# Attention and experts in one kernel: products as two column halves, experts' work in even shares, and the last batch's turns on TensorE

## The chip, the cores and the metric

The kernel runs on one core of one Trainium2 chip. The metric is the device time of the whole kernel in microseconds, as the median of several runs. All data are 32-bit floats.

The core has engines that run side by side and wait for each other by semaphores: TensorE (PE, with its weight loads PEld), VectorE (DVE), ScalarE (ACT), GpSimd (POOL) and SyncE (SP), which here only issues transfers. A "record" is one instruction in the profile; a 32-bit matmul leaves two records, each with a weight load of its own.

## The reference

The input x is 8 batches of 512 tokens with 256 channels. It is normalised over the channels. Two things are computed from the normalised tokens and added to x.

```python
xn = _layernorm(x, axis=-1)
x = x + attention(xn, qkv_w, out_w, bias_p, bias_a, rope_freqs) + experts(xn, Wg, w1, w2)

# attention: 16 heads of 64
qkv = (x @ qkv_w.T).reshape(Bb, Ss, 3, H, D)
q = _rope(q, c, s); k = _rope(k, c, s)
scores = einsum('bhqd,bhkd->bhqk', q, k) * SCALE
kb = -p * log1p(a * dist)                    # bias by distance, one p and a per head
attn = softmax(scores + kb[None], axis=-1)
out = einsum('bhqk,bhkd->bhqd', attn, v)  ->  out @ out_w.T

# experts: 16, each takes at most 256 tokens; a token goes to its best one
gate = softmax(xr @ Wg); idx = argmax(gate); loc = place of the token in its expert's queue
h = relu(einsum('ecm,emf->ecf', dispatched, w1))     # 256 -> 1024
expert_out = einsum('ecf,efm->ecm', h, w2)           # 1024 -> 256
combined = expert_out[idx, min(loc, C - 1)] * (gates_s * (loc < C))[:, None]
```

## The kernel before

**Steps and duos.** The 16 heads form 4 groups of 4, and a *step* s is one group on one batch: 32 steps, group by group over the 8 batches. A step has two *pairs* of heads. For each pair there are four blocks of 128 queries (`qc`); a pair with one block is a *unit*, and two units are a *duo* (`d`). So a step has four duos (`dd` 0 to 3), and the main loop runs over 128 duos. The order on every engine is the order in which the program issues instructions; no scheduler changes it.

**What one duo issues**, in this order:

- `project_qk` (matmuls L574) makes q or k of one pair for the next step: 128x128 weights, 512 columns of data. DVE shuffles the result (L578), ACT copies it (L583), and POOL rotates it by three operations (L587 to L589).
- `score` (L624) for the units of the next duo. Each head has its own 64 rows of the array. DVE adds the bias and reduces (L635), ACT takes the exponential and sums it (L639).
- `attend` (L716) in every second duo (`dd` 1 and 3), for a pair whose exponentials were turned some four duos before. Each head has 64 columns of the array. `attended` (L726) multiplies by the inverse sums on DVE.
- `project_out` (L755) for step s-2 in `dd` 0, twice; `project_v` (L601) in `dd` 0 and 1. The output is gathered in a tile y that is loaded from and stored to memory once in a step (`load_y`, `store_y`).
- `turn` (L648): DVE transposes blocks of 32x32 in the tile z of exponentials. When a pair is complete, `move` (L661) issues 16 transfers on SP's queue that put the blocks in their places (`pt<-z`), and three more (`rd`, `rb`) that spread the inverse sums.
- From duo 44 or so on, pieces of the experts' work (`expert_work`). An expert has 8 pieces of about the same size: four of `expert_hidden` (L519) and four of `expert_out` (L534). `expert_in` transposes an expert's tokens by TensorE (L504). How many pieces a duo takes is written out by hand:

```python
            for _ in range((1, 1, 4, 2 + s % 2)[dd]):
```

Weights of the experts are loaded by SP too; calls that issue them wait in a list `later`, which the next duo empties after `attend`.

**PSUM.** The pool `ps_mm` has two buffers for all products, `ps_sc` four for scores, `ps_av` and `ps_po` one each.

**The end.** From duo `late` (108) on, experts' results are gathered on POOL (L769), weighted on ACT (`weigh`, L781) and added on POOL (`combine`, L785). The last step's second pair is not moved by transfers: `turn_last` scales z by the inverse sums on DVE (L684), TensorE transposes it in blocks of 128x128 (L690), and ACT copies the result (L691). The first pair of the last step goes the ordinary way, through `turn`, `move` and `attend`, and is attended only when the loop is over. Then come `attend_last` (L705), the last `project_out`, and two stores (L983).

Of the kernel before, what the change touches and what calls it, by code (L numbers as in the profile page):

```python
# [37 lines left out]
def attention_and_experts(  # L38
# [138 lines left out]
    def rotation(stage):  # L177

        c1, c2 = 6.28125, 0.00193500518798828125
        c3 = 2.0 * math.pi - c1 - c2  # L180
        magic, edge = 12582912.0, 3.1415925
        n, r, away = two[0][:, 1, :], two[1][:, 0, :], two[1][:, 1, :]
        if stage == 0:
            nc.vector.tensor_scalar(n, ang, 0.5 / math.pi, magic, ALU.mult, ALU.add)
            nc.vector.tensor_scalar(n, n, magic, None, ALU.subtract)
            nc.vector.scalar_tensor_tensor(r, n, -c1, ang, ALU.mult, ALU.add)
        if stage == 1:
            nc.vector.scalar_tensor_tensor(r, n, -c2, r, ALU.mult, ALU.add)
            nc.vector.scalar_tensor_tensor(r, n, -c3, r, ALU.mult, ALU.add)
            nc.vector.tensor_scalar(r, r, edge, -edge, ALU.min, ALU.max)  # L190
            nc.scalar.activation(sin_t, r, AF.Sin, scale=sgn)

            nc.scalar.activation(away, r, AF.Abs)
            nc.scalar.activation(cos_t, away, AF.Sin, bias=quarter, scale=-1.0)


    mv = const.tile([P, NT, 2], F32, name="mv")
# [313 lines left out]
    def expert_hidden(e, f2):  # L511
        if f2 == 0:
            held["hT", e] = ffn["a"].tile([P, F // P, CAP], F32, tag="hT", name=f"hT_{e}")
        hT, xdT = held["hT", e], held["xdT", e]
        ph = ps_mm.tile([P, 2, CAP], F32, tag="mm", name=f"ph_{e}_{f2}")
        for i in range(2):
            fc = 2 * f2 + i
            for mc in range(2):
                nc.tensor.matmul(  # L519
                    ph[:, i, :],  # L520
                    held["w1", e, fc // 4][:, mc, (fc % 4) * P : (fc % 4 + 1) * P],
                    xdT[:, mc, :],
                    start=(mc == 0), stop=(mc == 1),
                )
        nc.scalar.activation(hT[:, 2 * f2 : 2 * f2 + 2, :], ph, AF.Relu)  # L525

    def expert_out(e, quarter):
        c, half = divmod(quarter, 2)
        hT = held["hT", e]
        if quarter == 0:  # L530
            held["po", e] = ps_po.tile([P, 2, DM], F32, tag="po", name=f"po_{e}")
        po = held["po", e]
        for fc in range(half * 4, half * 4 + 4):
            nc.tensor.matmul(  # L534
                po[:, c, :], hT[:, fc, c * P : (c + 1) * P], held["w2", e, fc // 4][:, fc % 4, :],
                start=(fc == 0), stop=(fc == F // P - 1),
            )
        if quarter == 3:
            ot = ffn["a"].tile([P, 2, DM], F32, tag="eo", name=f"eot_{e}")
            nc.scalar.copy(ot, po)  # L540
            later.append(
                lambda: nc.sync.dma_start(
                    eo[e * CAP : (e + 1) * CAP, :].rearrange("(c p) m -> p c m", p=P), ot
                )
            )

    def expert_work():
        for e in range(E):
            for f2 in range(4):
# [5 lines left out]
                yield  # L555
            for quarter in range(4):
                expert_out(e, quarter)
                if quarter == 2 and e + 1 < E:
                    expert_in(e + 1)
                if quarter == 3 and e + 1 < E:  # L560
                    later.append(lambda e=e: load_w2(e + 1))
                yield


    qk: dict = {}
    vals: dict = {}

    def project_qk(s, pair, part, turn_too=True):
# [2 lines left out]
        ps = ps_mm.tile([P, S], F32, tag="mm", name=f"qk_{s}_{pair}_{part}")  # L571
        c0 = part * GC + pair * P
        for mc in range(2):
            nc.tensor.matmul(  # L574
                ps, wq[:, mc, c0 : c0 + P], xnTs[s][:, mc, :], start=(mc == 0), stop=(mc == 1),
            )
        sh = rope.tile([P, S], F32, tag="sh", name=f"sh_{s}_{pair}_{part}", bufs=3)
# [13 lines left out]
    def project_v(s, i2):  # L591
# [6 lines left out]
        for i in range(2):  # L598
            c0 = (2 * i2 + i) * P
            for mc in range(2):  # L600
                nc.tensor.matmul(  # L601
                    ps[:, i, :], xnTs[s][:, mc, c0 : c0 + P], wq[:, mc, 2 * GC :],
                    start=(mc == 0), stop=(mc == 1),
                )
# [9 lines left out]
    def score(s, pair, qc):  # L614
# [1 line left out]
        g = s // B  # L616
        q, k = qk[s, pair, 0], qk[s, pair, 1]
        if qc == 0:
            zts[s, pair] = zpool.tile([P, TB, TB, 2, TB, 32], F32, tag="z", name=f"z_{s}_{pair}")
            sums[s, pair] = small.tile([P, 2, TB], F32, tag="sums", name=f"sums_{s}_{pair}")  # L620
        sc = [ps_sc.tile([P, S], F32, tag="sc", name=f"sc_{s}_{pair}_{qc}_{j}") for j in range(2)]
        for j in range(2):
# [6 lines left out]
            )  # L629
        st = small.tile([P, 2], F32, tag="st", name=f"st_{s}_{pair}_{qc}")  # L630
        for j in range(2):
            z = zts[s, pair][:, :, :, j, qc, :]
            bias = kb[g * HG + 2 * pair + j][:, :, TB - 1 - qc : 2 * TB - 1 - qc, :]

            nc.vector.tensor_tensor_reduce(  # L635
# [37 lines left out]
        pts[s, pair] = pt  # L673
        norms[s, pair] = rb

    def turn_last(s, pair, qc):

        if qc == 0:
            pts[s, pair] = zpool.tile([P, 2, TB, S], F32, tag="z", name=f"pt_{s}_{pair}")
        rs = small.tile([P, 2], F32, tag="rs", name=f"rs_{s}_{pair}_{qc}")  # L680
        nc.vector.reciprocal(rs, sums[s, pair][:, :, qc])
        for j in range(2):
            zn = rope.tile([P, S], F32, tag="sh", name=f"zn_{s}_{pair}_{qc}_{j}", bufs=3)
            nc.vector.tensor_scalar(  # L684
                zn.rearrange("p (c g k) -> p g c k", g=TB, k=32),
                zts[s, pair][:, :, :, j, qc, :], rs[:, j : j + 1], None, ALU.mult,
            )
            ps = ps_mm.tile([P, TB, P], F32, tag="mm", name=f"zt_{s}_{pair}_{qc}_{j}")
            for kc in range(TB):
                nc.tensor.transpose(ps[:, kc, :], zn[:, kc * P : (kc + 1) * P], ident)  # L690
            nc.scalar.copy(pts[s, pair][:, j, :, qc * P : (qc + 1) * P], ps)  # L691

    oTs: dict = {}
    avs: dict = {}

    def attend_last(s, pair, i2):

        if i2 == 0:
            avs[s, pair] = ps_av.tile([P, S], F32, tag="av", name=f"av_{s}_{pair}")
            oTs[pair] = qkpool.tile([P, S], F32, tag=f"o{pair}", name=f"o_{s}_{pair}", bufs=1)  # L700
        av, c = avs[s, pair], slice(i2 * 2 * P, (i2 + 1) * 2 * P)
        for kc in range(TB):
            for j in range(2):
                c0 = pair * P + j * D
                nc.tensor.matmul(  # L705
                    av[j * D : (j + 1) * D, c], vals[s][:, kc, c0 : c0 + D],
                    pts[s, pair][:, j, kc, c], start=(kc == 0), stop=(kc == TB - 1),
                )
        nc.vector.tensor_copy(oTs[pair][:, c], av[:, c])

    def attend(s, pair):
        avs[s, pair] = av = ps_av.tile([P, S], F32, tag="av", name=f"av_{s}_{pair}")
# [33 lines left out]
            out[b].rearrange("(n p) d -> p n d", p=P) if last else yd[b], ys.pop(s)  # L746
        )

    def project_out(s, i2):
        _, wot = weights[s // B]  # L750
        ps = ps_mm.tile([P, 2, DM], F32, tag="mm", name=f"po_{s}_{i2}")
        for i in range(2):
            c0 = (2 * i2 + i) * P
            for pair in range(2):
                nc.tensor.matmul(  # L755
                    ps[:, i, :], oTs[pair][:, c0 : c0 + P], wot[:, pair, :],
                    start=(pair == 0), stop=(pair == 1),
                )
        y = ys[s][:, 2 * i2 : 2 * i2 + 2, :]
# [40 lines left out]
        )  # L800


    steps = NG * B
    units = [(s, pair, qc) for s in range(steps) for pair in range(2) for qc in range(TB)]
    duos = len(units) // 2
    late = duos - 5 * TB
# [43 lines left out]
    turned_at = {3: 2, 6: 3, 8: 4, 10: 5, 12: 6, 14: 7}  # L850
    routing = route()
    working = begin = None
    for d in range(duos):
        s, dd = divmod(d, TB)
        g, b = divmod(s, B)
        pair, half = divmod(dd, 2)
        final = (s, pair) == units[-1][:2]
        if s + 1 < steps:
            project_qk(s + 1, *divmod(dd, 2))
        if d in turned_at:  # L860
            transpose_normed(turned_at[d])
        if d + 1 < duos:
            score(*units[2 * d + 2])
            score(*units[2 * d + 3])
        was = divmod((d - 5) // 2, 2) if half and d >= 5 else None
        if was:
            attend(*was)
# [13 lines left out]

        if dd == 0 and s > 1:
            project_out(s - 2, 0)
        if d == duos - 1:
            attended(*was)
            project_out(s - 1, 0)
            project_out(s - 1, 1)
            store_y(s - 1, True)
        (turn_last if final else turn)(*units[2 * d])
        if was and d < duos - 1:  # L890
            attended(*was)
        if d == 1:
            turn_logits(0)
# [3 lines left out]
            turn_logits(turned_at[d - 1])  # L897
        if dd in (0, 1):
            project_v(s, dd)
        (turn_last if final else turn)(*units[2 * d + 1])  # L900
        if dd == 1 and 4 <= s + 2 < steps:
            load_normed(s + 2)
        if half and not final:
            move(s, pair)
        if dd == 0 and s > 1:
            project_out(s - 2, 1)
# [26 lines left out]
            expert_in(0)  # L933
            working = expert_work()
        elif working:
            for _ in range((1, 1, 4, 2 + s % 2)[dd]):
                if working and next(working, True):
                    working = None

        assert working is None or d < late  # L940

        if d >= late and s < steps - 1:
            if dd < 2:
                gather(b - 1, dd)
            if dd == 2:
# [28 lines left out]
                bias_tables(g + 1, 0, 1)  # L974
        if b == 0 and g > 0 and dd == 0:
            bias_tables(g, 1, 1)
    attend(s, 0)
    attended(s, 0)
    for i2 in range(2):
        attend_last(s, 1, i2)  # L980
    for i2 in range(2):
        project_out(s, i2)
        nc.sync.dma_start(  # L983
            out[B - 1, i2 * 2 * P : (i2 + 1) * 2 * P].rearrange("(n p) d -> p n d", p=P),
            ys[s][:, 2 * i2 : 2 * i2 + 2, :],
# [50 lines left out]
```

## Time and profile before

| | |
|---|---|
| median of 3 runs | 1260.9 us (1260.34 to 1262.82) |
| the profiled execution | 1259.97 us |
| its span, first to last instruction | 1258.3 us |
| PE busy | 1214.7 us, 97% of the span |
| DVE busy | 892.5 us, 71% |
| ACT, POOL busy | 611.8 us, 618.1 us |
| mean granted TensorE clock | 0.990 |
| PE idle from 1150 to 1200 us | 4.3 of 50 us |
| transfers | 264.15 MB, mean 210 GB/s |

The busy time of PE counts its matmul records, which overlap each other; the gap between the starts of two groups tells more than their length. A row of the chain gives the start in us, the length in us, and the engine with the line and the number of instructions. In a row of the timeline the bracket gives the time for which the engine stood idle before it, and what released it. SPq is the time that SP needs to issue transfers.

The main groups of matmuls, with their shape (rows x columns of the array, then rows x columns of data):

| line | what | shape | records | busy us |
|---|---|---|---|---|
| L624 | scores | 64*128, 64x512 | 1024 | 254.7 |
| L574 | q and k | 128*128, 128x512 | 512 | 246.4 |
| L716 | attention times v | 128*64, 128x512 | 1008 | 232.1 |
| L755 | output product | 128*128, 128x256 | 512 | 124.4 |
| L601 | v | 128*128, 128x256 | 512 | 124.1 |
| L534 | experts, second product | 128*128, 128x256 | 512 | 120.3 |
| L519 | experts, first product | 128*128, 128x256 | 512 | 118.7 |

### The profile page before, as it was taken

The numbers are of one execution on the slowest core, as the hardware profiler recorded it, in microseconds if no ns is written. First come the engines' busy times: TensorE is split into PE (matmuls) and PEld (weight loads), VectorE is DVE, ScalarE is ACT, GpSimd is POOL, SyncE is SP. The second block draws the span as 40 slices with busy tenths as digits, with TensorE's granted clock in tenths as the row PEclk, the third lists the DMA queues.
The fourth block names the chain that finished last, engine by engine and source line by source line (L and its number), as shares of the span: only waits on it lengthen the run. The fifth ranks groups of instructions, "written<-read, shape, count | busy, mean of one in ns | idle before, by whom it ended". The sixth has DMA issues, their size and how long they took to land.

```text
span 1258.3 us, 17383 instructions
## 1 busy us (share of the span) xinstructions
PE 1214.7 (97%) x5070; PEld 669.1 (53%) x5070; DVE 892.5 (71%) x2265; ACT 611.8 (49%) x1425; POOL 618.1 (49%) x614
## 2 busy tenths in 40 slices
PE   8799999999999999999999999999999999998977
PEld 5344444444465656656565665655656554444444
DVE  7988899999966656555656566655665668888762
ACT  6565655566443444335543344443446435555550
POOL 5766754555543444334443344433434335687850
PEclk9899999999999999999999999999999999999988
DMA  4489998888888997778786787877778768889995
GB/s 135 146 219 262 253 252 203 207 218 208 212 240 210 239 265 193 198 198 212 199 232 166 237 202 211 227 196 205 195 196 215 191 166 203 220 229 218 246 232 139
DMA packets 152414, 264.15 MB, mean 210 GB/s; under 512 B 32176, under 2 KB 96448, under 8 KB 152320
## 3 DMA queue, kind: packets, MB, share of 16 engines
q1 hardware_dynamic: 144848, 240.98, 72.5%
q0 software_dynamic: 6368, 20.99, 5.8%
q10 hardware_dynamic: 1104, 1.07, 0.2%
q8 instruction: 41, 0.67, 0.2%
q14 instruction: 53, 0.43, 0.1%
HBM read 99.39 MB, written 31.44 MB: 104 GB/s over the span
## 4 chain that ended last, share of the span: by engine, by line
PE 76%; DVE 8%; DMA 7%; SPq 4%; POOL 2%; ACT 2%; issue 1%; ACTq 0%; DVEq 0%; POOLq 0%
PE sc L624 15%; PE qk L574 14%; PE av L716 14%; PE ph L519 9%; PE po L534 9%; PE v L601 7%; PE po L755 7%; SPq L661 3%; DVE z L635 3%; DMA pt<-z 2%; DVE z L648 2%; DMA rd<-turned 1%; DMA xnT<-xnd 1%; DMA xnd<-xnT 1%; DMA out<-early 1%
## 5 line engine op out<-in xcount | busy, mean ns | idle before, releaser
L587 POOL TENSOR_TENSOR t<-t,cos_t 128x512 f32<-128x512 f32 (+1 forms) x126 | 161.3, 1280 | 537.9 <-ACT t L583 537.4
L639 ACT ACTIVATE z<-z,st 128x512 f32<-128x512 f32 x512 | 363.4, 712 | 35.2 <-DVE st L635 26.0
L635 DVE CUSTOM_DVE_ANT_1 z<-sc,kb 128x512 f32<-128x512 f32 x512 | 322.5, 686 | 29.2 <-PE sc L624 23.8
L648 DVE STREAM_TRANSPOSE z<-z 128x512 f32<-128x512 f32 x504 | 319.9, 682 | 0.0
L624 PE MATMUL sc<-t,t 64*128 64x512 f32 x1024 | 254.7, 616 | 0.7 <-DVE t L589 0.7
L574 PE MATMUL qk<-xnT,wq 128*128 128x512 f32 x512 | 246.4, 604 | 6.5 <-ACT early L781 1.9
L716 PE MATMUL av<-pt,v 128*64 128x512 f32 x1008 | 232.1, 602 | 3.7 <-DMA rb<-rd 1.8
L583 ACT COPY t<-qk 128x512 f32<-128x512 f32 x125 | 73.2, 585 | 330.6 <-DVE sh L578 324.3
L624 PEld LDWEIGHTS sc<-t,t 64*128 64x128 f32 x1024 | 88.3, 186 | 154.1 <-issue 124.3
L578 DVE LOAD_MASK_SELECT sh<-qk x128 | 1.8, 14 | 231.6 <-PE qk L574 224.7
L589 POOL TENSOR_TENSOR t<-t,sh 128x512 f32<-128x512 f32 (+1 forms) x126 | 160.6, 1275 | 9.9
L588 POOL TENSOR_TENSOR sh<-sh,sin_t 128x512 f32<-128x512 f32 (+1 forms) x126 | 161.2, 1279 | 0.0
L716 PEld LDWEIGHTS av<-pt,v 128*64 128x64 f32 x1008 | 67.8, 137 | 159.6 <-issue 131.3
L574 PEld LDWEIGHTS qk<-xnT,wq 128*128 128x128 f32 x512 | 93.8, 191 | 95.2 <-issue 67.5
L755 PE MATMUL po<-wo,o 128*128 128x256 f32 x512 | 124.4, 386 | 0.4 <-ACT t L583 0.2
L601 PE MATMUL v<-wq,xnT 128*128 128x256 f32 x512 | 124.1, 385 | 0.0
L534 PE MATMUL po<-w,hT 128*128 128x256 f32 x512 | 120.3, 383 | 1.0 <-ACT hT L525 1.0
L519 PE MATMUL ph<-xdT,w 128*128 128x256 f32 x512 | 118.7, 382 | 1.4 <-ACT eot L540 1.4
L755 PEld LDWEIGHTS po<-wo,o 128*128 128x128 f32 x512 | 94.4, 190 | 36.9 <-issue 12.6
L601 PEld LDWEIGHTS v<-wq,xnT 128*128 128x128 f32 x512 | 94.7, 190 | 35.8 <-DVE z L648 13.8
L519 PEld LDWEIGHTS ph<-xdT,w 128*128 128x128 f32 x512 | 95.7, 190 | 26.5 <-ACT z L639 4.9
L534 PEld LDWEIGHTS po<-w,hT 128*128 128x128 f32 x512 | 95.2, 190 | 25.3 <-issue 8.7
(147 smaller groups left out, 831.9 us busy)
## 6 DMA issues: line engine op xcount, KB each, us to landing
pt<-z SPq DMA_DIRECT2D x1008, 128.0 KB
w<-in_w SPq DMA_DIRECT2D x64, 512.0 KB
rb<-rd SPq DMA_DIRECT2D x126, 128.0 KB
xnT<-xnd SPq DMA_DIRECT2D x28, 512.0 KB
yd<-y SPq DMA_DIRECT2D x26, 512.0 KB
y<-yd SPq DMA_DIRECT2D x24, 512.0 KB
xrd<-xn POOLq DMA_DIRECT2D x8, 512.0 KB
xnd<-xnT POOLq DMA_DIRECT2D x8, 512.0 KB
```

The source lines that it names most:

```text
L519: nc.tensor.matmul(ph[:, i, :], held["w1", e, fc // 4][:, mc, (fc % 4) * P : (fc % 4 + 1) * P], xdT[:, mc, :], start=(mc == 0), stop=(mc = ...
L534: nc.tensor.matmul(po[:, c, :], hT[:, fc, c * P : (c + 1) * P], held["w2", e, fc // 4][:, fc % 4, :], start=(fc == 0), stop=(fc == F // P ...
L574: nc.tensor.matmul(ps, wq[:, mc, c0 : c0 + P], xnTs[s][:, mc, :], start=(mc == 0), stop=(mc == 1),)
L587: eng.tensor_tensor(t[:, c], ps[:, c], cos_t[:, c], ALU.mult)
L588: eng.tensor_tensor(sh[:, c], sh[:, c], sin_t[:, c], ALU.mult)
L601: nc.tensor.matmul(ps[:, i, :], xnTs[s][:, mc, c0 : c0 + P], wq[:, mc, 2 * GC :], start=(mc == 0), stop=(mc == 1),)
L624: nc.tensor.matmul(sc[j].rearrange("p (g c k) -> p g c k", g=TB, k=32), q[r, qc * P : (qc + 1) * P], k[r, :].rearrange("p (c g k) -> p g c ...
L635: nc.vector.tensor_tensor_reduce(z, sc[j].rearrange("p (g c k) -> p g c k", g=TB, k=32), bias, -0.125, 3.0e38, ALU.add, ALU.min, st[:, j : ...
L639: nc.scalar.activation(z, z, AF.Exp, bias=st[:, j : j + 1], scale=-1.0, accum_out=sums[s, pair][:, j, qc : qc + 1],)
L648: nc.vector.transpose(z, z)
L716: nc.tensor.matmul(av[j * D : (j + 1) * D, :].rearrange("p (a q) -> p a q", q=P), vals[s][:, kc, c0 : c0 + D], pts[s, pair][:, :, kc, j, : ...
L755: nc.tensor.matmul(ps[:, i, :], oTs[pair][:, c0 : c0 + P], wot[:, pair, :], start=(pair == 0), stop=(pair == 1),)
```

## The change

It has three parts.

1. A new function `product` stands in for the single matmul in `project_qk`, `project_v`, `project_out`, `expert_hidden` and `expert_out`. It issues two matmuls, one for each half of 64 columns of the weights, on the same data; the halves fill the two halves of the output's partitions. The transposes keep all 128 columns.
2. The pieces of the experts' work are spread by a running count, so that the last one falls in the last duo before `late`. `expert_in` of the next expert is called from the list `coming`, behind the scores of the duo that follows its piece `quarter` 0; before, it was called at `quarter` 2, among the pieces.
3. The loop ends four duos earlier, and the last step is written out behind it. Both pairs of it are now transposed by TensorE straight from the exponentials (`turn_last`), half of the copies back by ACT and half by DVE, in place. The inverse sums are not multiplied in before: `sums_last` widens them on DVE, `spread_last` turns them by TensorE into the layout of the output, and `attend_last` multiplies by them at the end. So that the keys may keep their order, a copy of the last step's input is reordered by ACT (`reordered`), and v is made from that copy.

```diff
+    def product(o, w, v, start, stop):
+
+        for c in range(2):
+            half = slice(c * D, (c + 1) * D)
+            nc.tensor.matmul(o[half], w[:, half], v, start=start, stop=stop)
...
             for mc in range(2):
-                nc.tensor.matmul(
+                product(
                     ph[:, i, :],
...
             for quarter in range(4):
                 expert_out(e, quarter)
-                if quarter == 2 and e + 1 < E:
-                    expert_in(e + 1)
+                if quarter == 0 and e + 1 < E:
+                    coming.append(e + 1)
...
-    def turn_last(s, pair, qc):
-
-        if qc == 0:
-            pts[s, pair] = zpool.tile([P, 2, TB, S], F32, tag="z", name=f"pt_{s}_{pair}")
-        rs = small.tile([P, 2], F32, tag="rs", name=f"rs_{s}_{pair}_{qc}")
-        nc.vector.reciprocal(rs, sums[s, pair][:, :, qc])
+    def turn_last(s, pair, qc, spare=(ps_po, "po")):
+
+
         for j in range(2):
-            zn = rope.tile([P, S], F32, tag="sh", name=f"zn_{s}_{pair}_{qc}_{j}", bufs=3)
-            nc.vector.tensor_scalar(
-                zn.rearrange("p (c g k) -> p g c k", g=TB, k=32),
-                zts[s, pair][:, :, :, j, qc, :], rs[:, j : j + 1], None, ALU.mult,
-            )
-            ps = ps_mm.tile([P, TB, P], F32, tag="mm", name=f"zt_{s}_{pair}_{qc}_{j}")
-            for kc in range(TB):
-                nc.tensor.transpose(ps[:, kc, :], zn[:, kc * P : (kc + 1) * P], ident)
-            nc.scalar.copy(pts[s, pair][:, j, :, qc * P : (qc + 1) * P], ps)
+            z = zts[s, pair][:, j, qc].rearrange("p g c k -> p g (c k)")
+            pool, tag = spare if j else (ps_mm, "mm")
+            ps = pool.tile([P, TB, P], F32, tag=tag, name=f"zt_{s}_{pair}_{qc}_{j}")
+            for g in range(TB):
+                nc.tensor.transpose(ps[:, g], z[:, g], ident)
+            (nc.vector.tensor_copy if j else nc.scalar.copy)(z, ps)
+
+    def sums_last(s, pair):
+
+        inv = inverse[pair]
+        nc.vector.reciprocal(inv[:, : 2 * TB], sums[s, pair].rearrange("p j c -> p (j c)"))
+        norms[s, pair] = rope.tile([P, 2, TB, D], F32, tag="sh", name=f"wide_{pair}", bufs=3)
+        nc.vector.tensor_copy(
+            norms[s, pair].rearrange("p j c d -> p (j c) d"),
+            inv[:, : 2 * TB].unsqueeze(2).to_broadcast([P, 2 * TB, D]),
+        )
+
+    def spread_last(s, pair):
+
+        wide = norms[s, pair]
+        ps = ps_po.tile([P, S], F32, tag="po", name=f"spread_{pair}")
+        for qc in range(TB):
+            for j in range(2):
+                nc.tensor.matmul(
+                    ps[j * D : (j + 1) * D, qc * P : (qc + 1) * P], wide[:, j, qc, :], ident,
+                    start=True, stop=True,
+                )
+        norms[s, pair] = rope.tile([P, S], F32, tag="rb", name=f"rb_{s}_{pair}")
+        nc.scalar.copy(norms[s, pair], ps)
...
-    for d in range(duos):
+    for d in range(duos - TB):
...
+        if s == steps - 2 and dd == 2:
...
+            reordered = xpool.tile([P, 2, S], F32, tag="xnT", name="reordered")
...
+        while coming:
+            expert_in(coming.pop())
...
-            for _ in range((1, 1, 4, 2 + s % 2)[dd]):
+            share = (1, 1, 4, 2)
+            due = 8 * E * sum(share[k % TB] for k in range(begin + 1, d + 1)) / sum(
+                share[k % TB] for k in range(begin + 1, late))
+            for _ in range(min(4, math.ceil(due - 1e-6) - pieces)):
+                pieces += 1
                 if working and next(working, True):
                     working = None
...
+    s, rest = steps - 1, units[-2 * TB :]
+    xnTs[s] = reordered
+    score(*rest[2])
+    score(*rest[3])
...
+    for unit in rest[:2]:
+        turn_last(*unit)
+    weigh(B - 2)
+    gather(B - 1, 1)
+
+    score(*rest[4])
+    score(*rest[5])
+    attend(s - 1, 0)
+    load_y(s)
+    attended(s - 1, 0)
+    for unit in rest[2:4]:
+        turn_last(*unit)
+    sums_last(s, 0)
...
+    score(*rest[6])
+    score(*rest[7])
+    spread_last(s, 0)
+    attend_last(s, 0, 0, TB)
+    for unit in rest[4:6]:
+        turn_last(*unit)
+    combine(B - 1, ys[s])
+    attend(s - 1, 1)
+    attended(s - 1, 1)
+    turn_last(*rest[6], (ps_sc, "sc"))
+    sums_last(s, 1)
+    turn_last(*rest[7], (ps_sc, "sc"))
+    for i2 in range(2):
+        project_out(s - 1, i2)
+    store_y(s - 1, True)
+    spread_last(s, 1)
+    for i2 in range(2):
+        attend_last(s, 1, i2, 2)
     for i2 in range(2):
-        project_out(s, i2)
+        project_out(s, i2, lasts)
```

## The prediction

> **What bounds the kernel now.** I read the page's engine row and chain first, then stretches of the span, then the chain row by row where it changes, then the end.
>
> ```profile
> PE 1214.7 (97%) x5070; PEld 669.1 (53%) x5070; DVE 892.5 (71%) x2265; ACT 611.8 (49%) x1425; POOL 618.1 (49%) x614
> PE 76%; DVE 8%; DMA 7%; SPq 4%; POOL 2%; ACT 2%; issue 1%; ACTq 0%; DVEq 0%; POOLq 0%
> ```
> TensorE is the bound on average. By stretches (us, then busy time of PE, PEld, DVE, ACT, POOL, then granted clock, DMA share, GB/s):
>
> ```profile
> 200.00:400.00 200.00, 198.42 (x822) 97.48 (x821) 175.76 (x454) 104.35 (x245) 101.12 (x83) 1.00 0.86 218
> 600.00:800.00 200.00, 200.00 (x831) 121.86 (x828) 120.72 (x292) 87.79 (x200) 81.69 (x68) 1.00 0.76 208
> 1150.00:1200.00 50.00, 45.69 (x176) 20.31 (x172) 40.49 (x100) 28.39 (x72) 40.05 (x34) 1.00 0.99 251
> 1225.00:1258.00 33.00, 25.14 (x120) 14.29 (x120) 6.91 (x14) 4.23 (x8) 2.35 (x1) 0.86 0.53 143
> ```
> From 60 to 1119 us PE is never free: only less PE time helps. Near 1150 the DMA share is 0.99 and PE waits for transfers. At the end PE has gaps and a lower clock. Now the chain where PE carries it (start, length, instructions):
>
> ```profile
> 1140.75 1.73 PE v L601 x8
> 1142.47 1.73 PE po L755 x8
> 1144.20 1.72 PE qk L574 x4
> 1145.92 1.92 PE sc L624 x8
> 1147.83 3.58 PE av L716 x16
> 1151.42 1.93 PE v L601 x8
> ```
> The same v group takes 1.73 us behind another full 128x128 group but 1.93 behind av, which uses 64 columns. sc (64 rows) takes 1.92 where its eight records at 0.215 make 1.72; av takes 3.58 where sixteen make 3.44. So each change of the array's shape costs PE 0.20 us, or 0.145 where the weights entered have only 64 columns. Last, PE's timeline at the end:
>
> ```profile
> 1208.16 3.65 PE L716 MATMUL av<-pt,v 128*64 128x512 f32 x16 [0.66 <-issue]
> 1218.10 1.57 PE L690 MATMUL zt<-ident,zn 128*128 128x128 f32 x8 [2.45 <-DVE zn L684]
> 1225.37 1.97 PE L690 MATMUL zt<-ident,zn 128*128 128x128 f32 x8 [5.70 <-ACT pt L691]
> 1227.27 4.37 PE L716 MATMUL av<-pt,v 128*64 128x512 f32 x16
> 1245.64 1.95 PE L705 MATMUL av<-pt,v 128*64 128x256 f32 x16 [0.80 <-DVE o L726]
> ```
> Gaps, and behind them slow groups: the av of 3.65 us takes 4.37 after the 5.70 us gap.
>
> **Part one: products as two halves of 64 columns.** A product of 128 output rows becomes two matmuls on halves of the array's columns. av already has this form: in the starts of its records two stand 7 ns apart and pairs follow every 429 ns, and the full qk records also follow every 429 ns. For 256 columns of data L705 shows 16 records in 1.95 us against 1.93 for eight full v records, both behind other work; pairs follow every 216 ns, full ones every 216. So the work itself costs nothing more, though PE issues 7694 matmul records instead of 5070.
>
> What changes is the number of shape changes. I counted them along PE's instruction order in both kernels. Leaving a 64-column group for a full one: 62 before, 21 after, so 41 x 0.20 = 8.2 us less. Leaving a full group for a 64-column one: 2 before, 32 after, 30 x 0.145 = 4.4 us more; these are the transposes (expert inputs, normed batches, logits), which stay full and used to stand among full products. Score groups followed by 64-column work: 61 before, 104 after, 43 x 0.055 = 2.4 us less; after the logits 8 x 0.055 = 0.4 less. Net 6.6 us less. Expert inputs moved behind sc, out of the experts' work, are in this count at 15 x 0.20 = 3.0 us of loss.
>
> A rule speaks against it. The Trainium skill, "TensorE: Matmul & The Clock Gate", section "What overlaps and what doesn't", says that a weight load runs beside matmuls in flight only if its row group differs. Both halves use all 128 rows, so by the rule their loads would not be hidden. The two 64-column loads of a pair would cost, at the 0.137 us of the av loads' row, up to 0.27 us on each of 2560 pairs: 700 us slower. The starts in L716 and L705, 429 and 216 ns a pair with each pair's loads between, show them hidden. I take the trace. What no row shows is two halves reading the same data at once; its bounds are 0 and the rule's 0.27 us, and I take 0 because av is the same form in all but that.
>
> **Part two: experts' work spread.** The 128 pieces run to the last duo allowed, three duos later than before; PE is full in both stretches, so moving pieces costs nothing. Each step now has the pattern 1, 1, 4, 2, so a new expert always opens a new duo. Before, PE waited twice 0.69 us for an expert's output copy where one expert followed another at once (818 and 862 us): 1.4 us less. Transposes of an expert's input now wait for its gather on POOL, issued two duos earlier; their copy stands on DVE behind four score reductions (4 x 0.61 us), while PE has av or po (1.7 to 3.6 us) and one more PSUM buffer. If that cover fails a step loses under 1 us. SP stores the last expert output just before POOL gathers; POOL then waits a few us with rope work behind it that is needed two duos (14 us) later: 0. The weights of w1 are asked for in duo four and used at the end of the next duo, some 16 us; 1 MB at the 208 GB/s of that stretch is 5 us: 0.
>
> **From 1119 us the gain stops.** There the chain is SP's issues and transfers:
>
> ```profile
> 1176.33 2.94 SPq L661 DMA_DIRECT2D pt<-z  x4
> 1179.93 11.32 SPq L661 DMA_DIRECT2D pt<-z  x12
> 1191.29 1.30 SPq L669 DMA_DIRECT2D rb<-rd  x2
> ```
> Twelve issues took 11.3 us where a free run of them takes 7.50 (the one at 1196.88), and av at 1194.63 waited 1.75 us for rb. The change leaves these queues alone, so PE's 0.5 us a step over 2.5 steps becomes waiting: 1.2 us lost. Up to 1194.63: 6.6 + 1.4 - 1.2 = 6.8 us less.
>
> **Part three: the last batch.** From that av to the end took 63.7 us: 41.8 us of PE work at full pace, 12.1 of gaps, 4.5 from the last matmul to the end (DVE 0.69, transfer 3.8), and the rest, 5.3, is the lower clock. The change removes the last batch's first pair's 16 pt, 1 rd and 2 rb issues on SP (1225.3 to 1237.7), 8 DVE transposes of 0.68 and 8 scalings of 0.48. It adds 32 transposes of 0.109 us (from the xdp group, 0.437 for four), 32 records that spread the sums (1.7 us), two ACT copies that reorder the last input (0.6 each, beside 44% of ACT's time), and 8 copies on DVE of about 0.69 (the row of xdT). PE's work becomes 47.1 us.
>
> Waits on that path: the last pt of the batch before (SP issues it to 1222.96, its buffer was free at 1224.7) is wanted by my sum at about 1225.7 on the same scale, just in time. Single-buffered turns wait for a DVE copy three times at about 0.4: 1.2 us. Other hand-overs, 0.9. The y of the last batch, asked for 12 us earlier on SP, lands and is added with about 6 us to spare. The slow groups stood behind gaps of 2.45 and 5.70 us; none as long is left in my sum, so I expect the full clock, and the 5.3 us go with the 12.1 of gaps. 47.1 + 2.1 + 4.5 = 53.7 against 63.7: 10.0 us less.
>
> **Sum.** 6.8 + 10.0 = 16.8 us from the profiled execution's 1259.97 us (span 1258.3 and 1.7 around it): 1243.2. The profiled run lies 0.9 under the median of 1260.9 and inside the runs' range, so I say 1243.5.
>
> **Rivals.**
> A: transfers hold the end (0.2). If the last pt arrives when it did before, whatever PE saved, av of the batch before waits 6 to 7 us in the new end. For: DMA share 0.99 and the tight meeting above. Against: the queue's backlog begins only near 1119, so it should shift with PE. About 1249.
> B: halves are not free (0.06). If each pair costs over 6.6 ns more than one full product, 2560 pairs eat the whole 16.8 us. At 20 ns, 51 us: 1294. For: same-data reads and 50% more records are shown nowhere. Against: L716 and L705 agree with full products to 1 ns.
> C: the even pattern frees more (0.12): fewer waits on transfers near 1130 to 1195, where PE stood idle 6.2 us, because fewer steps run there without experts. About 1237.
> D: the switch saving isn't real, or new expert waits of 0.5 us in each of 15 steps eat it (0.1): the end alone, about 1250.
>
> **Numbers.** The main case has 0.52, range 1239 to 1248. With A whole and the larger part of C and D the range is 1236 to 1252; outside lie B, the far ends of C and D, and a twelfth or so of the main case. Within 0.2% is what this measurement can't tell from no change, 2.5 us: only a small part of B and D reaches it. Faster 0.92, same 0.02, slower 0.06.
>
> **What would show it.** Right: v behind av 1.73 us; sc still 1.92; po behind sc about 1.87; a steady step without experts 28.9 us instead of 29.4; pairs every 216 ns; granted clock 1.0 to the last us; no PE gap over 2 us after 1190. Wrong: product pairs above 220 ns, PE waiting at xdp once a step, or a gap of several us before av near the end with pt as releaser.

## The result, and the profile after

The changed kernel takes 1252.15 us (median of 5 runs, 1248.99 to 1254.39) against 1260.34 us for the kernel before (5 runs, 1257.51 to 1262.82): a ratio of 0.992, 95% interval 0.9895 to 0.9946. It is faster by about 8 us by the medians and 10 by the ratio, where the forecast was 17. The time lies outside the prediction's main range (1239 to 1248) and at the edge of its wide one (1236 to 1252). The profiled execution took 1253.45 us, with a span of 1251.7.

The page after: the engine row, the chain by engine, and the row of qk (busy us, mean ns of one | idle just before, releaser).

```profile
PE 1212.5 (97%) x7694; PEld 559.8 (45%) x7694; DVE 889.6 (71%) x2255; ACT 613.3 (49%) x1429; POOL 617.6 (49%) x614
PE 80%; DMA 8%; SPq 4%; DVE 3%; ACT 2%; issue 1%; POOL 1%; ACTq 0%; DVEq 0%
...
L200 PE MATMUL qk<-xnT,wq 128*64 128x512 f32 x1024 | 245.4, 600 | 13.4 <-DMA xnT<-xnd 8.7
```

Half as many records again, and PE is no busier. The halves of qk cost 245.4 us where the whole products cost 246.4. What is new stands behind the second bar: qk now waits 8.7 us for xnT, the load of the next normed batch. In the kernel before no such wait was listed.

The chain where PE carries it, after (start, length, instructions):

```profile
1109.50 1.88 PE po L200 x16
1111.37 1.73 PE v L200 x16
1113.10 1.73 PE po L200 x16
1114.83 1.72 PE qk L200 x8
1116.54 1.92 PE sc L635 x8
1118.46 3.58 PE av L749 x16
1122.05 1.73 PE v L200 x16
```

v behind av takes 1.73 us instead of 1.93, sc still takes 1.92, and po behind sc 1.88: these are the savings that the prediction counted. The next view is PE's waits over the whole span (engine, line, what it waited for: us in total, times, longest).

```profile
PE qk L200 <- DMA xnT<-xnd: 8.7, 6, 2.7
...
PE qk L200 <- ACT z L650: 2.5, 1, 2.5
PE zt L695 <- issue: 2.3, 1, 2.3
PE xdp L510 <- DMA xg<-xrd,sidx: 2.1, 1, 2.1
...
PE po L200 <- DMA w<-in_w: 1.2, 1, 1.2
```

2.7 of the 8.7 us fall at 1164 us. Without them and the row of zt, 11.8 us of waits lie in the middle, between 190 and 565 us. So PE did become quicker, and stood waiting for what it had gained. Two of these waits cost more than their length: behind the one for xg (at 385.75 us) and the xnT one at 1164 the granted clock was 0.79 and 0.76 (from 384 to 392 and from 1166 to 1173 us), and the qk behind the second took 2.50 us instead of 1.94. Last, PE's timeline from the last but two av on (start, length, group [idle before it <- releaser]).

```profile
1194.21 3.65 PE L749 MATMUL av<-pt,v 128*64 128x512 f32 x16 [0.47 <-DMA rb<-rd]
...
1206.89 1.79 PE L695 MATMUL zt<-ident,z 128*128 128x128 f32 x12
1211.00 0.66 PE L695 MATMUL zt<-ident,z 128*128 128x128 f32 x4 [2.32 <-issue]
1211.59 3.26 PE L635 MATMUL sc<-t,t 64*128 64x512 f32 x8
1214.78 4.03 PE L749 MATMUL av<-pt,v 128*64 128x512 f32 x16
...
1230.11 3.65 PE L749 MATMUL av<-pt,v 128*64 128x512 f32 x16
```

The gap of 5.70 us is gone. One of 2.32 is there, and behind it sc takes 3.26 us instead of 1.99. Nearly the whole gain of the span lies here. The last but two av starts 0.42 us earlier than before (1194.63), and the rest of the kernel takes 57.5 us from there instead of 63.7.

### The profile page after: what moved, and what is told of

Its sections match the earlier page's. It is cut to its first block, busy times and chain, and to the rows that moved or that the text cites. A ratio compares the mean times of both kernels' runs of the same rounds, so it can differ in the third digit from the quotient of the medians.

```text
span 1251.7 us, 22571 instructions
## 1 busy us (share of the span) xinstructions
PE 1212.5 (97%) x7694; PEld 559.8 (45%) x7694; DVE 889.6 (71%) x2255; ACT 613.3 (49%) x1429; POOL 617.6 (49%) x614
## 4 chain that ended last, share of the span: by engine, by line
PE 80%; DMA 8%; SPq 4%; DVE 3%; ACT 2%; issue 1%; POOL 1%; ACTq 0%; DVEq 0%
PE po L200 18%; PE sc L635 16%; PE qk L200 15%; PE av L749 14%; PE v L200 8%; PE ph L200 7%; DMA xnT<-xnd 3%; SPq L672 3%; DMA pt<-z 2%; DMA w<-in_w 2%; ACT xn L255 1%; DVE z L646 1%; PE xdp L510 1%; ACT z L650 1%; PE zt L695 1%
## 5 line engine op out<-in xcount | busy, mean ns | idle before, releaser
L200 PE MATMUL qk<-xnT,wq 128*64 128x512 f32 x1024 | 245.4, 600 | 13.4 <-DMA xnT<-xnd 8.7
L200 PEld LDWEIGHTS qk<-xnT,wq 128*64 128x64 f32 x1024 | 71.2, 137 | 118.5 <-issue 83.1
L200 PE MATMUL po<-wo,o 128*64 128x256 f32 x1024 | 122.5, 382 | 0.0
L200 PE MATMUL po<-w,hT 128*64 128x256 f32 x1024 | 118.4, 380 | 1.4 <-DMA w<-in_w 1.2
L200 PE MATMUL v<-wq,xnT 128*64 128x256 f32 x992 | 117.8, 380 | 0.0
L200 PE MATMUL ph<-xdT,w 128*64 128x256 f32 x1024 | 117.5, 380 | 0.0
L650 ACT ACTIVATION_READ_ACCUMULATOR z<-z,st 128x1 f32 x512 | 95.8, 187 | 0.0
L587 DVE STREAM_SHUFFLE sh<-qk 128x512 f32<-128x512 f32 x128 | 93.8, 733 | 0.7
L200 PEld LDWEIGHTS po<-wo,o 128*64 128x64 f32 x1024 | 70.8, 137 | 52.1 <-ACT t L592 8.3
L200 PEld LDWEIGHTS po<-w,hT 128*64 128x64 f32 x1024 | 72.5, 137 | 47.8 <-issue 7.4
```

The lines of the kernel that those rows point to most:

```text
L200: nc.tensor.matmul(o[half], w[:, half], v, start=start, stop=stop)
L587: nc.vector.stream_shuffle(sh, ps, ROT)
L650: nc.scalar.activation(z, z, AF.Exp, bias=st[:, j : j + 1], scale=-1.0, accum_out=sums[s, pair][:, j, qc : qc + 1],)
```

## Where the middle's gain went

The trace gives the start of each step's first score group. As differences to the kernel before in us (the runs are those of the experiments below):

| step | before starts at | after | products alone (e1) | last batch's part alone (e2) | after, xnT on GpSimd (e4) | before, xnT on GpSimd (e5) |
|---|---|---|---|---|---|---|
| 5 | 185.05 | +0.28 | -0.50 | -1.45 | -0.59 | +0.20 |
| 8 | 275.30 | +1.29 | -0.38 | -0.48 | -1.31 | +0.20 |
| 10 | 336.98 | +4.23 | +2.79 | +1.13 | -1.58 | +0.21 |
| 28 | 1098.12 | +2.17 | -0.23 | +1.93 | -9.72 | +0.54 |
| 31 | 1190.89 | +0.86 | +3.18 | +2.39 | -12.85 | -3.49 |

Between steps 11 and 27 the experts' work lies in different places in the kernels, so the rows are taken where none is in hand. At step 28, with all of it done, the changed kernel is 2.2 us late where the forecast has it about 8 early (6.6 for shape changes and 1.4 for the experts' meetings). By step 10, before any expert's work, it is already 4.2 us late. One stretch of the span, from 276 to 308 us, before and then after (us, busy time of PE, PEld, DVE, ACT, POOL, granted clock, DMA share, GB/s):

```profile
276.00:308.00 32.00, 31.43 (x129) 14.00 (x128) 31.93 (x83) 22.04 (x50) 21.21 (x18) 1.00 0.86 213
```

```profile
276.00:308.00 32.00, 29.45 (x170) 11.85 (x168) 31.43 (x81) 22.11 (x48) 20.98 (x18) 1.00 0.80 201
```

PE is busy 1.98 us less in the same 32 us. That is idle time, and more than the 0.5 us that its work shrank by in a step. DMA is less busy too, so nothing here says that the bandwidth gave out. DVE, in the same rows, was busy 31.93 of 32 us before; the experiment e4 comes back to that. SP's own timeline in that stretch, after:

```profile
276.84 0.33 SPq L778 DMA_DIRECT2D yd<-y  x1
277.28 0.36 SPq L245 DMA_DIRECT2D xnT<-xnd  x1
277.74 2.83 SPq L672 DMA_DIRECT2D pt<-z  x4
280.67 0.53 SPq L677 DMA_DIRECT2D rd<-turned  x1
281.25 9.58 SPq L672 DMA_DIRECT2D pt<-z  x12
```

A free run of twelve pt issues takes 7.50 us; these take 9.58. The records of the trace name the semaphore on which each transfer reports that it has landed. SP takes eight of them in turn:

```
start   semaphore  transfer
277.28  107        xnT<-xnd
277.74  109        pt<-z
278.71  111        pt<-z
279.35  112        pt<-z
279.98  113        pt<-z
280.67  114        rd<-turned
281.25  115        pt<-z
281.80  116        pt<-z
284.60  107        pt<-z, which first waits for semaphore 107
```

The eighth issue behind xnT has to wait until xnT is in. Seven issues of about 0.63 us are gone by in 5 us. The load needs 7.3, so SP stands for 2.2. The same holds for each y load. SP's waits from 185 to 345 us, before and then after:

```profile
SPq L661 <- DMA xnT<-xnd: 10.5, 6, 2.5
SPq L661 <- DMA y<-in_x: 6.9, 4, 2.3
```

```profile
SPq L672 <- DMA xnT<-xnd: 10.7, 5, 2.4
SPq L672 <- DMA y<-in_x: 7.0, 4, 2.0
```

The stalls were there before too, and cost nothing in that trace: SP took 30.1 to 31.2 us from one xnT to the next, and PE's steps took as long (29.9 to 31.0). SP's other waits in that stretch before (for DVE and PE) add to about 6.5 us in five steps, so it had some 1.3 us a step in hand. Now PE's work is 0.5 us a step less. At 282.2 PE wants the batch whose load left SP at 277.28 and lands at 284.6. (The profile puts this wait of 2.5 us down to ACT z, which ended at 284.69; but PE goes on at 284.72, 0.14 us behind the landing at 284.58, as it does behind the other xnT loads.) SP comes to that load late because of its stalls, and then stalls behind it again; from one xnT to the next it now takes 30.5 to 32.5 us. Why it fell behind its own earlier pace, and not only down to it, the runs do not settle. PE's saving is not needed for it, as e2 shows below. A wait on PE delays the scores from which SP's next transfers come, so that the two can wait in turn; that is argued, not shown.

## The experiments

Each ratio is to the kernel before, run beside it on the same chip (its medians there: 1261.8 to 1262.9 us). The first four share one chip, the next four a second, the last two a third. The changed kernel itself was measured on none of these, so comparisons with it go by the ratios.

**One part at a time.** e1 is the kernel before with only its five products made into halves:

```diff
+    def product(o, w, v, start, stop):
+        for c in range(2):
+            half = slice(c * D, (c + 1) * D)
+            nc.tensor.matmul(o[half], w[:, half], v, start=start, stop=stop)
```

> The kernel before with the products as two halves of 64 columns, and nothing else of the change. Theory T (SP's queue sets the pace where no expert runs: eight transfers may be outstanding, a 512 KB one is waited for eight issues later, so a step needs 30 to 31 us of SP whatever PE does): the switches saved show only in the stretch with experts and in the last steps before 1119 us, and PE waits for xnT between 185 and 345 us as in the changed kernel; the expert inputs stay among the products here and cost two switches each. About 1256 us, 3 to 5 less than before. Rival S (the switch sum holds everywhere, what was lost was lost by the new shares): 6 to 7 us less, and no wait for xnT over 0.5 us. Rival H (halves are not free): not faster, product pairs over 220 ns.

Measured: 1259.95 us, ratio 0.9975 (0.996 to 0.9989), about 3 us faster. PE's waits in it:

```profile
PE qk L201 <- DMA xnT<-xnd: 11.4, 5, 4.0
```

A step without experts took 28.91 us instead of 29.40 in the trace, so the saving is real, and xnT takes most of it.

e2 has the last batch's new part alone: whole products, and the experts' shares and the place of their inputs as before.

```diff
     def product(o, w, v, start, stop):
-        for c in range(2):
-            half = slice(c * D, (c + 1) * D)
-            nc.tensor.matmul(o[half], w[:, half], v, start=start, stop=stop)
+        nc.tensor.matmul(o, w, v, start=start, stop=stop)
...
+            for _ in range((1, 1, 4, 2 + s % 2)[dd]):
```

> The kernel before with the last step in its new form alone; whole products and the old shares. The end took 57.0 us from the last-but-two av on in the changed kernel and 63.7 before, so T expects about 6.5 us less than before, 1254, with all of it behind 1190 us. If the new end needs the halves to pay (shape changes around its transposes), 5 or less. If the whole gain of the change came from elsewhere, no difference.

Measured: 1253.36 us, 0.994 (0.9919 to 0.9961). From the last but two av (1195.75) to the end of its span (1250.1) it took 54.4 us, against 63.7 before: the part for the last batch does alone about what it was forecast to do. The gap before the last zt of the first group was 0.3 us here.

Its trace holds something else. Up to its last steps e2 issues the same instructions in the same order as the kernel before, on every engine. Yet PE waits for xnT in it:

```profile
219.78 1.96 PE L198 MATMUL qk<-xnT,wq 128*128 128x512 f32 x4 [0.55 <-DMA xnT<-xnd]
250.95 1.96 PE L198 MATMUL qk<-xnT,wq 128*128 128x512 f32 x4 [1.73 <-DMA xnT<-xnd]
281.57 1.95 PE L198 MATMUL qk<-xnT,wq 128*128 128x512 f32 x4 [1.18 <-ACT z L648]
312.66 1.95 PE L198 MATMUL qk<-xnT,wq 128*128 128x512 f32 x4 [1.46 <-ACT z L648]
```

The last two also end 0.14 us behind the landing of xnT (281.43 and 312.53). That is 4.9 us in four steps with whole products, where the trace of the kernel before has none. It came to step 5 1.45 us ahead and lost 2.6 us up to step 10. So SP can hold the middle of the kernel before as well, from one execution to another.

e3 is the changed kernel with the old shares and the old place of the experts' inputs:

```diff
-            share = (1, 1, 4, 2)
-            due = ...
-            for _ in range(min(4, math.ceil(due - 1e-6) - pieces)):
-                pieces += 1
+            for _ in range((1, 1, 4, 2 + s % 2)[dd]):
...
-                if quarter == 0 and e + 1 < E: coming.append(e + 1)
+                if quarter == 2 and e + 1 < E: expert_in(e + 1)
```

> The changed kernel with the old shares of the experts' pieces and the old place of the expert inputs. T: the new shares start the experts faster while SP is behind and cost about 2 to 4 us at the first expert; undone, these return, while waits of 0.69 us where experts meet come back too: within 3 us of the changed kernel, 1249 to 1252. Rival S (the shares lost what the switches gained): 5 us or more faster than the changed kernel, 1246 or less.

Measured: 1257.85 us, 0.9961 (0.9945 to 0.9977), 5 us more than the changed kernel by the ratios, which is more than the 3 expected. Not all of that is the shares: in its profile the gap before zt was longer, with slow groups behind it, and from the first scores of the last step on it takes 3.6 us longer than the changed kernel.

```profile
1207.83 1.80 PE L695 MATMUL zt<-ident,z 128*128 128x128 f32 x12
1214.46 1.11 PE L695 MATMUL zt<-ident,z 128*128 128x128 f32 x4 [4.83 <-DVE z L696]
1215.50 3.79 PE L635 MATMUL sc<-t,t 64*128 64x512 f32 x8
```

**Take the suspected load off SP.** e4 is the changed kernel with one word changed:

```diff
-        nc.sync.dma_start(xnT, xnd[s % B])
+        nc.gpsimd.dma_start(xnT, xnd[s % B])
```

> The changed kernel with the load of the normed input (xnT, 512 KB, one in a step) issued by GpSimd and no longer on SP's queue. T: the waits of PE for xnT between 185 and 345 us (7 us in the profile of the changed kernel) go, SP's stall of about 2 us behind each xnT goes, and the kernel gains 6 to 9 us, 1243 to 1246. Rival (transfers as such are the bound there, at a DMA share near 0.85, and not SP's order): the load only comes late by another queue, no gain, 1250 to 1253. GpSimd has room: 49% busy; but its rotations stand behind the load, which could cost up to 1 us in a step.

Measured: 1240.71 us, 0.9845 (0.9817 to 0.9873). SP's waits from 185 to 345 us, and then PE's over the whole span:

```profile
SPq L672 <- DMA y<-in_x: 6.0, 4, 1.7
SPq L672 <- DMA yd<-y: 3.0, 3, 1.5
```

```profile
PE qk L200 <- DVE y L794: 3.2, 6, 1.6
PE zt L695 <- DVE z L696: 1.8, 3, 1.0
...
PE av L749 <- DMA pt<-z: 1.6, 1, 1.6
```

No wait for xnT is left on either engine. The start of step 31 comes 12.85 us earlier than before, and the same transfers were made.

One part of the middle did not gain as counted. From step 5 to step 10 this run gains 1.0 us (-0.59 to -1.58), where five steps at 0.49 us make 2.4, and e6 gains the same 1.0. The stretch, in e4:

```profile
185.00:337.00 152.00, 149.91 (x874) 59.49 (x870) 147.06 (x383) 84.97 (x200) 84.45 (x71) 1.00 0.84 215
```

DVE is busy for 147.06 of the 152 us, and PE waits there 1.1 us for DVE and 0.8 for ACT. With SP out of the way DVE is probably the next to hold PE; no run tests it.

e5, e6 and e7 make the same edit in the kernel before, in e1 and in e3. They ask whether the load had held the kernel before as well, and what each part is worth once it doesn't.

> The kernel before with the xnT load on GpSimd's queue and nothing else. If SP's queue already held the kernel before (steps of 30 to 31 us between 185 and 345 us where PE's work is 29.4, and the waits for transfers after 1119 us), this alone gains: T expects 3 to 6 us, about 1257. If PE held it, as the prediction said, no gain.

> The kernel before with halves as products and the xnT load on GpSimd's queue. By T the switch sum shows in full once SP does not set the pace: against the kernel before with the load moved, 0.5 us less in each of 31 steps, less 0.34 for each of 15 expert inputs that stand among halves here, less about 3 us early: 7 us less. Without the load moved it was 3 us.

> The changed kernel with the xnT load on GpSimd's queue, and the old shares with the old place of the expert inputs. The prediction's sum gives the new shares 15 x 0.145 us for the inputs standing behind the scores and 1.4 us for waits where experts meet: 3 to 4 us slower than the same kernel with the new shares. If the shares matter only through SP's queue, no difference.

| with xnT on GpSimd | us | ratio | interval | beside the one above |
|---|---|---|---|---|
| e5: before | 1254.71 | 0.9942 | 0.9921 to 0.9963 | |
| e6: and products as halves | 1252.55 | 0.9914 | 0.9886 to 0.9943 | -0.28%, 3.5 us |
| e7: and the last batch's part | 1244.66 | 0.9863 | 0.9837 to 0.9888 | -0.51%, 6.5 us |
| e4: and the experts' shares | 1240.71 | 0.9845 | 0.9817 to 0.9873 | -0.18%, 2.3 us |

Neighbouring intervals overlap, so the small steps are rough sizes and no more; by the medians, which e5 to e7 share a chip for, the first two are 2.2 and 7.9 us. The halves were expected to give 7 us in e6 and gave half of that. In the trace of e5 each step starts 0.2 to 0.5 us later than in that of the kernel before until 1127 us (last column of the table above), and its gain comes after that, where the prediction already had SP and transfers in the chain. So between these two executions SP held nobody in the middle. But their spans are only 3.2 us apart and the medians 7.3 (the traced run of e5 is its slowest), and in e2 the same middle did wait. How much the load costs the kernel before in its middle stays open. The whole change is worth e4 over e5, 0.9902, some 12.4 us, where it was worth 0.992, some 10, with the load on SP (by the medians some 15 and 8). So the load on SP explains a part of what is missing from the forecast of 16.8, and not all of it.

e8 moves the y loads to GpSimd as well:

```diff
-        nc.sync.dma_start(ys[s], ...)
+        nc.gpsimd.dma_start(ys[s], ...)
```

> The changed kernel with the loads of xnT and of y, two of 512 KB in a step, on GpSimd's queue. T: SP loses another stall of about 2 us and 0.6 us of issue in a step, so the waits left between 1100 and 1195 us go: 1 to 4 us less than with xnT alone moved, 1237 to 1240. Rival: GpSimd's queue now waits for y's buffer with rotations behind it, or the transfers themselves are the bound by now (DMA share near 0.9): no gain, or up to 3 us slower.

Measured: 1250.15 us, 0.9905 (0.9878 to 0.9932): slower than e4 by 7.6 us by the ratios, more than even the rival said. PE's waits point to a part of the reason:

```profile
PE lgp L301 <- DVE nt L219: 9.2, 1, 9.2
...
PE xdp L510 <- DMA xg<-xrd,sidx: 4.0, 4, 1.3
PE po L200 <- ACT t L592: 3.8, 3, 2.8
```

POOL issues in its order too. At 374.74 us a y load had waited 1.5 us there for its buffer, and the first expert gathers (xg), for which PE then waited, stood behind it; near the end another waited 8.0 us. That is a part of the loss. 3.9 us of it are there by step 5, from the row of lgp at the start, where no y load waits; why, the run does not show.

**Which: a late load, or the turn of eight?** e9 puts the load on ACT, so that it is off SP's queue but, if the eight semaphores are shared, still in their turn:

```diff
-        nc.sync.dma_start(xnT, xnd[s % B])
+        nc.scalar.dma_start(xnT, xnd[s % B])
```

> The changed kernel with only the normed batch's load (xnT) issued by ACT in place of SP. Theory (SP is the second queue that paces the kernel: behind each 512 KB load its next issues stall about 2 us, and the load itself leaves SP some 14 us after its buffer is free): with SP rid of it the waits of qk for xnT go, and the time is that of the run with the load on GpSimd, ratio 0.9845 to the kernel before, 1241 us, within 2 us. Rival 1 (the stall lies with completions that SP and ACT take in common turn, and only GpSimd is outside of it): SP still stalls some 2 us behind each load, though the load itself leaves early; PE's waits for xnT go but SP stays close behind; 0.987 to 0.990, 1246 to 1250 us. Rival 2 (a wait for the buffer on ACT holds the exps behind it): PE waits for ACT before sc or qk once a step, 0.3 to 0.5 us each; 1247 us or more.

Measured: 1335.1 us (1331.13 to 1340.64), 1.0579 (1.0532 to 1.0626). All three figures were wrong, but the mechanism is the first rival's, and stronger. (The 14 us are misread, too: in the changed kernel the loads of this stretch leave SP 4.6 to 6.2 us after PE's last read of their buffer.) SP's waits over the whole span of e9:

```profile
SPq L672 <- DMA xnT<-xnd: 120.5, 22, 14.8
...
SPq L672 <- DMA w<-in_w: 56.2, 36, 4.5
...
SPq L680 <- DMA xnT<-xnd: 21.2, 2, 12.8
```

SP waits 142 us for a load that it doesn't issue. The records show how, around one of the worst:

```
start   queue  semaphore  transfer
411.15  SP     114        pt<-z
411.70  SP     115        pt<-z
416.13  ACT    116        xnT<-xnd
419.53  SP     116        pt<-z, which first waits for semaphore 116
```

In this program SP and ACT draw from one turn of eight, laid down in the order of the program. SP was at its place in the turn by 412.3, and ACT's load, which had semaphore 116 before it, was issued only at 416.13 because ACT had to come through its own work first. SP stood for 7.2 us, partly for a transfer that had not begun. The weights of the experts leave SP late by as much, and PE waits for them: 24.6 us at ph and 20.4 at po. In e4 the semaphores of SP go round without the load's, and no such wait is there.

**The gap before zt.** e10 is e4 with one line moved, the last gather behind the next scores and av:

```diff
     weigh(B - 2)
-    gather(B - 1, 1)
...
     attended(s - 1, 0)
+    gather(B - 1, 1)
```

> The changed kernel with the xnT load on GpSimd, and the last gather of the last batch's expert rows (four indirect issues on POOL) put behind the next two score groups, the av and its output copy. It asks whether those issues are what makes the transposes of the last batch wait over 2 us for a copy that began late (2.32 us at 1208.68 in the changed kernel; 1.17 and 1.01 with the load moved). If they are: the gaps before zt fall to the 0.4 us that were forecast, 1.4 us less, 1239 us, ratio 0.983. If they aren't: gaps of 1 us or more stay somewhere before zt, 1240 to 1242 us, 0.984 to 0.986. If weighing the gathered rows then holds ACT behind a gather that lands late: ACT waits some us for room, 1243 us or more.

Measured: 1239.38 us, 0.982 (0.979 to 0.985), the lowest median of the study. Its timeline:

```profile
1195.53 1.53 PE L695 MATMUL zt<-ident,z 128*128 128x128 f32 x12 [1.10 <-DVE y L794]
1197.48 0.65 PE L695 MATMUL zt<-ident,z 128*128 128x128 f32 x4 [0.41 <-issue]
...
1205.51 0.66 PE L695 MATMUL zt<-ident,z 128*128 128x128 f32 x4 [0.42 <-DVE z L696]
```

The gap of 1.0 us that e4 had before the last transposes of its second group is 0.42 here. The 1.1 before the first group is a wait for the residual add on DVE and stayed. But the span is 1237.6 us beside e4's 1237.8, and the intervals of the two overlap. So the question stays open. With the gather in one place the longest gap before a group's last transposes was 2.32 us in the changed kernel, 0.7 in e2, 4.83 in e3, 1.0 in e4 and 0.4 in e7, so that one profile with it moved proves little. What the changed kernel shows is that the copies of the turned blocks on DVE and ACT began at 1210.25 and 1210.96, at least 1.6 and 2.3 us after PE's last record of them (1208.68), where 0.3 is usual. Both engines stood idle until then, by the trace for PE.

## Why the prediction came out as it did

**Right: the shape changes and the halves.** v behind av, sc and po behind sc measured 1.73, 1.92 and 1.88 us, and a step without experts 28.91 in e1 instead of 29.40, each as forecast. The rule that the prediction weighed (the Trainium skill, "TensorE: Matmul & The Clock Gate", "What overlaps and what doesn't": a load runs beside matmuls only if its row group differs) does not describe these halves: they share all rows, the profile gives their loads 71.2 us for qk, and yet a qk of halves takes 1.72 us in the chain, as a whole one did, and PE's busy time for qk fell by 1.0 us. Rival B is out.

**Wrong: "From 60 to 1119 us PE is never free: only less PE time helps".** That was read off PE's busy time, and the conclusion doesn't follow: a full engine says that the others are not slower, not by how much they are quicker. SP was within about 1.3 us a step of PE from 185 to 345 us, so close that in e2 it held PE with no saving at all, and in the changed kernel and e1 it took what was saved. The prediction looked for SP only where it already stood in the chain, from 1119 us on. So the term "Up to 1194.63: 6.8 us less" measured 0.4 us less. With the load on GpSimd, where PE no longer waits for it, step 28 starts 9.7 us earlier beside the 8.0 that the same terms make: the sum came out, and the queue beside it was what was missing. That the sum came out so well is in part luck: from step 5 to step 10 only 1.0 of 2.4 us showed, and DVE was nearly full there. The prediction's own row for 200 to 400 us has DVE at 175.76 of 200 us, and it counted no wait for DVE in the middle.

**Right, with a new cost: experts' work.** The two meetings of 0.69 us are gone. The costs put at 0 were not all 0 while SP was late: an expert's input was waited for once (2.1 us) and weights once (1.2 us). With the load moved the shares are worth 2.3 us.

**The end: right in kind, 3.8 us too good.** Forecast 53.7 us, measured 57.5.

| | forecast | measured |
|---|---|---|
| PE at work | 47.1 | 50.0 |
| PE waiting | 2.1 | 3.7 |
| last matmul to the end | 4.5 | 3.8 |

The y of the last batch and the pt of the batch before were in time: the av at 1230.11 shows no wait, so Rival A did not come about. The wait of 2.32 us, which the sum took as one of three of 0.4, is the miss in the second row. Of the 2.9 us in the first, 1.7 are the slower groups behind it (sc 3.26 for 1.99, av 4.03 for 3.65); the rest was not traced. The prediction expected the full clock because no gap as long as 2.45 us was left, and the row for that stretch shows otherwise:

```profile
1200.00:1225.00 25.00, 22.22 (x150) 11.62 (x148) 12.94 (x35) 14.00 (x35) 12.32 (x10) 0.93 0.86 223
```

In e2 and e4, whose gaps before zt were 0.7 and 1.2 us at most, the granted clock is 1.00 in that stretch and the groups behind took 1.99 and 3.65.

**The sum.** By the traces it missed by 6.4 us up to 1194.63 and by 3.8 at the end, 10.2 of the 16.8. The time landed near Rival D's 1250, "the end alone", but that is luck, for D's reasons are not the ones. The saving is real, and the experts' new waits are the smaller part of what ate it: the fault is a second resource that ran just behind the first.

## What to carry to other kernels

Before you credit a saving on the engine that is full, measure how far behind it the next one runs, step by step: its own period, its stalls included, not its waits for others. Do it for every engine and queue, and in more than one execution: the same middle waited 4.9 us in one trace here and not at all in another. A queue that issues many small transfers can be held up by the few large ones in it; look for a stall a fixed number of issues behind each large one, and move the large ones to a queue with room. Before moving one, see whether the other queue shares the turn of completion semaphores, and what stands in order behind the issue there.

## What the hardware showed that was not expected

- SP and ACT share one turn of eight completion semaphores in these programs. A 512 KB load that lands 7.3 us after its issue stalls the eighth issue behind it for 2.2 us. Issued by ACT, the same load held SP for 142 us in total and the kernel was 5.8% slower; issued by GpSimd it held SP for nothing and the kernel was 0.75% faster than with the load on SP (0.9845 against 0.992).
- Two 64-column halves that read the same data cost PE no more than the whole product: 245.4 us against 246.4 for qk, 1.72 us from start to start in both, with 50% more records overall and PE's total 2.2 us lower.
- A copy behind PE's transposes can start 1.6 to 2.3 us after their last record where 0.3 is usual. The runs do not settle why.
